# A decoder of twelve sub-layers on one core: a routed layer's first half placed beside the attention ahead of it, and two layers joined at their seam

## The chip, the cores and the metric

The kernel runs on one core of a Trainium2 chip. The core has a matrix engine (PE, TensorE), a vector engine (DVE, VectorE), an engine for activation functions (ACT, ScalarE), a general engine (POOL, GpSimd) and one that mainly issues transfers (SP, SyncE). Each takes its instructions in order from a queue of its own and waits for the others by semaphores. The metric is the device time of one execution in microseconds, the median of three runs.

## The reference

An input `x` of 32 sequences, 128 positions and 128 features goes through four decoder layers of three sub-layers each. Every sub-layer normalizes `x` and adds its result to `x`. Cut to the calls:

```
x = x + _L0_attn_ref(_layernorm(x), ...)        # state-space layer: convolution, gates, chunks of 64
x = x + _L0_xattn_ref(_layernorm(x), ctx, ...)  # cross attention, 8 heads of 64
x = x + _L0_ffn_ref(_layernorm(x), ...)         # mixture of 16 experts
x = x + _L1_attn_ref(...); x = x + _L1_xattn_ref(...); x = x + _L1_ffn_ref(...)
x = x + _L2_attn_ref(_layernorm(x), ...)        # one head
x = x + _L2_xattn_ref(ctx, _layernorm(x), ctx, ...)  # 16 heads, relative positions
x = x + _L2_ffn_ref(_layernorm(x), ...)         # top-1 mixture and a shared expert
x = x + _L3_attn_ref(_layernorm(x), ...)        # attention by sparsemax
x = x + _L3_xattn_ref(...); x = x + _L3_ffn_ref(...)
```

The mixture that matters here is the ninth sub-layer:

```
probs = softmax(x @ Wr)                         # 8 choices, 7 of them with an expert
p, ind = the largest of probs
out = 2.0 * p * sum over j < 7 of swiglu(x, Wu[j], Wg[j], Wd[j]) * (ind == j)
out = out + swiglu(x, Wu_s, Wg_s, Wd_s)         # the shared expert; hidden size 512
```

## The kernel before

`x` stays in SBUF as G=8 tiles, each one *group* of J=4 sequences: 128 positions on the partitions, 4x128 values beside each other. Each sub-layer is a function, `layer0` to `layer11`, called in order at the end of `program`; their matrices come as *units* of 768 KB in a pool of four buffers (tag `unit`). Other pools are named by what they hold: `bbig` (4 buffers) and `gbig` (3) of 2048 values a partition, `bmid` (5) and `gmid` (10) of 512, and in PSUM `ps`, `two` and `acc`, two buffers each.

The order of work is written out by hand. The wrapper `Ordered` (L181) keeps the instructions of VectorE, ScalarE and TensorE in the order of the program between `follow(T, A, V)` and `follow()`; that is why almost every row of the profile has the line L194 and groups are told apart by their tiles. GpSimd (`P`) and SyncE (`SY`) aren't wrapped; a scheduler places their instructions.

`layer0` works in rounds, one sequence in two chunks per round, G*J=32 in all. A round calls `first`, `second`, `third` and `weighted` for its chunks, and between them, by `go`, the next step of generators for other groups: `entry` (norm and turn), `conv` (convolution strand), `decays`, `gate`, and `joined` (gating, root mean square, projection, adding to `x`) for the group before. The loop runs from -9 to G*J+1, so that the first groups' preparation and the last group's `joined` are in rounds of their own.

`layer1` then prepares its first group and a half (`prepare`, `project_in`, `scores`, `project_values`) and runs 32 rounds of its own, with the next layer's preparation (`then`) in its last ones. `attention16` serves the 16-head attentions; it, too, works in rounds, one sequence each: transposes of the probabilities, scores of the next round, softmax, `weighted` (product with the values) of the round before, and one step of an iterator `others` handed to it. `layer7` is such an attention; its `others` were the leftovers of `layer6`.

`layer8` is the top-1 mixture. The tokens are dealt with in two halves (*sides*, four groups each). For one side: `ready` normalizes and `gate` makes logits, `route` picks the best expert by the routine `first_k`, `place` gives each token a row in DRAM so that an expert's rows stand in blocks of 256 (`TOKENS`), 14 tiles (`TILES`) in all; `send` scatters 128 tokens by an indirect transfer to `xs` (16 a side); `load(t)` gathers tile t's 768 KB of expert weights to a unit buffer; `rows` reads the tile's tokens back; `up` and `down` make the products and scatter the results to `ys`; `collect` reads them back and adds them. `shared` is a quarter of a group of the shared expert (16 pieces a side). `xs` and `ys` are filled with empty rows beforehand. `layer8_first` does all this for side 0, and routing and sending for side 1; side 1's tiles go to the list `beside`, which `layer9`, the sparsemax attention, takes up among its sorting steps.

Of the kernel before, what the change touches and what calls it, by code (L numbers as in the profile page):

```python
# [13 lines left out]
I8 = mybir.dt.int8  # L14
# [190 lines left out]
def program(ctx, tc, cols, x, ctxt, mask, drop, dfirst, dsmall, dwide, drows, dunits, dexperts, dconst, drel, dwq, out):  # L205
# [72 lines left out]
    SY.dma_start(out=cs, in_=dconst)  # L278
# [3 lines left out]
    for i in range(G):  # L282
# [3 lines left out]
        if i == 0:  # L286
            w0 = units.tile([128, cfirst.n], F32, tag="unit", name="w0")
            A.dma_start(out=w0, in_=dfirst)
            ww = const.tile([128, cwide.n], F32, name="ww")
            A.dma_start(out=ww, in_=dwide.to_broadcast([128, cwide.n]))  # L290
            wr = const.tile([1, crows.n], F32, name="wr")
            A.dma_start(out=wr, in_=drows)
# [26 lines left out]
    ctxT = [const.tile([128, 512], F32, name=f"ctxT{i}") for i in range(G)]  # L319

# [65 lines left out]
    def normed(i):  # L386

        xn = mid.tile([128, J, D], F32, tag="xn", name="xn", bufs=2)
# [7 lines left out]
        for j in range(J):  # L396
            P.tensor_scalar(xn[:, j, :], xg[i][:, j, :], mv[:, j, 0:1], rs[:, j : j + 1], ALU.subtract, ALU.mult)  # L397
# [270 lines left out]
    def layer0():  # L668
# [190 lines left out]
        def joined(g):  # L859

            ys, sq = [], []
            for b in range(2):
                y = bmid((128, J, 128))
# [8 lines left out]
            for y in ys:  # L872
                q = bmid((128, J, 128))
# [10 lines left out]
            ln = bmid((128, J, 128))  # L884
            A.copy(ln, op)
            yield
# [21 lines left out]
        for n in range(-9, G * J + 2):  # L908
# [46 lines left out]
            go(conv, g, c)  # L955
        follow()

    def layer1(then):  # L960
# [12 lines left out]
        def project_in(n):  # L973
            i, j = n // J, n % J
            at = slice(j * 128, (j + 1) * 128)
            if n % 2 == 0:
                keys[n // 2] = gbig((128, 2, 4, 256))
# [81 lines left out]
        follow(T, A, V)  # L1059
        prepare(0, 0)  # L1060
        prepare(0, 1)
        project_in(0)
        for c2 in range(2):
            for step in scores(0, c2):
                step()
        prepare(1, 0)
        project_in(1)
        project_values(0)
        for n in range(last + 1):
# [10 lines left out]
            if n < last:  # L1080
# [12 lines left out]
                weighted(n)  # L1093
                if j == 0 and 0 < i and i + 1 < G:
# [3 lines left out]
        follow()  # L1098
# [339 lines left out]
    def layer8(side):  # L1438

        N = G // 2  # L1440


        E = D + 1
        xs = dram.tile([TILES * TOKENS + HALF, E], F32, name=f"xs{side}", tag=f"xs{side}")
        ys = dram.tile([HALF + TILES * TOKENS, D], F32, name=f"ys{side}", tag=f"ys{side}")
        xs_rows = xs[0 : TILES * TOKENS].rearrange("(p n) e -> p n e", p=128)
        rows = TILES * TOKENS // 128
        number = small(rows)
        V.tensor_scalar(number[:, 0:1], K["row"], float(rows), float(HALF), ALU.mult, ALU.add)
        V.tensor_scalar(number, K["count"][:, 0:rows], number[:, 0:1], None, ALU.add)  # L1450
        for a in range(0, rows, 14):
            empty = bbig((128, 14, E))
            P.memset(empty, 0.0)
            V.tensor_copy(empty[:, :, D].bitcast(I32), number[:, a : a + 14])
            SY.dma_start(out=xs_rows[:, a : a + 14], in_=empty)
            if a == 0:
                SY.dma_start(out=ys[0:HALF].rearrange("(p n) d -> p n d", p=128), in_=empty[:, 0:1, 0:D].to_broadcast([128, HALF // 128, D]))
        xn_all = bbig((128, N, J, E))
        own = small(N * J)
        V.tensor_scalar(own, K["count"][:, 0 : N * J], 128.0, K["row"], ALU.mult, ALU.add)  # L1460
        V.tensor_copy(xn_all.rearrange("p n j e -> p (n j) e")[:, :, D].bitcast(I32), own)
# [3 lines left out]
        xnTs, sums, ins, mids = {}, {}, {}, {}  # L1465

        def ready(i):
            norm(xg[side * N + i], xn_all[:, i, :, 0:D])
# [482 lines left out]
```

## Time and profile before

| what | value |
|---|---|
| median of three runs | 3045.65 us (3045.08 to 3048.45) |
| profiled execution, its own time | 3068.78 us |
| its span, from first to last instruction | 3066.8 us |
| mean granted TensorE clock | 0.91 |
| busy: PE, DVE, ACT, POOL | 2563.0, 2086.1, 1529.3, 1007.4 us |
| bytes moved by DMA | 68.36 MB, mean 22 GB/s |
| attention of layer7, rounds 1 to 31 (VectorE's reciprocals of `weighted`) | 2039 to 2310 us |
| layer8 from the attention's last add to the last tile of side 0 | 2312.9 to 2504.4 us |

Busy times and shares are over the whole span. A row of a window has the start and end of a stretch and its length, then the busy time and the number of instructions of PE (matrix products), PEld (its weight loads), DVE, ACT and POOL, then the granted clock of PE (1 is full speed), the mean busy share of the DMA engines, and what they moved in GB/s. A row of the chain of waits has a start, a duration and what the kernel's end stood on at that time: an engine with its tile, "issue" where the engine waited for nothing that the profile shows, or "another core or an unknown queue". The kernel uses one core, so the latter is a queue here. All times of places are microseconds from the start of the span.

### The profile page before, as it was taken

What the parts mean: (1) busy time and instruction counts of PE and PEld (TensorE: products, weight loads), DVE (VectorE), ACT (ScalarE), POOL (GpSimd) and SP (SyncE); (2) the same over time, 40 slices, a digit from 0 to 9 for tenths busy, and PEclk for the clock granted to TensorE, in tenths of its full rate; (3) what the DMA queues carried; (4) which work ended last, traced back from release to release, by engine and by line L of the source; (5) the groups of instructions that cost most, each with busy time, mean ns of one, the idle gap of its engine ahead of it and who ended that gap; (6) DMA issues with size and microseconds to landing.
All of it is one profiled execution on the core that took longest, in us unless ns stands there. A gap on an engine that the chain in (4) does not pass through costs nothing.

```text
span 3066.8 us, 55735 instructions
## 1 busy us (share of the span) xinstructions
PE 2563.0 (84%) x22535; PEld 1638.7 (53%) x22554; DVE 2086.1 (68%) x4254; ACT 1529.3 (50%) x3540; POOL 1007.4 (33%) x1042
## 2 busy tenths in 40 slices
PE   4887878999989999999998999988886869885564
PEld 2555556777744445556664444445553657543333
DVE  4776756888878856667776555468894329777883
ACT  3554544444422246666664444467771225555563
POOL 3333332322310113235441000223433445424544
PEclk7877878999999999999998999979997989998777
DMA  3000000000000000000000000000003243100000
GB/s 109 2 2 2 2 23 4 8 5 5 1 21 1 1 32 2 5 9 9 12 2 15 1 1 1 1 1 2 1 6 124 84 147 114 55 18 14 21 11 21
DMA packets 50147, 68.36 MB, mean 22 GB/s; under 512 B 3681, under 2 KB 41570, under 8 KB 49762
## 3 DMA queue, kind: packets, MB, share of 16 engines
q1 hardware_dynamic: 42608, 33.84, 3.6%
q0 software_dynamic: 6848, 27.81, 2.7%
q8 instruction: 178, 2.92, 0.4%
q10 hardware_dynamic: 434, 3.14, 0.3%
q14 instruction: 79, 0.65, 0.1%
HBM read 51.11 MB, written 13.68 MB: 21 GB/s over the span
## 4 chain that ended last, share of the span: by engine, by line
PE 49%; DVE 31%; ACT 8%; POOL 6%; issue 3%; DMA 1%; another core or an unknown queue 1%; SPq 0%; POOLq 0%; DVEq 0%; ACTq 0%
PE ps L194 22%; PE two L194 15%; PE acc L194 13%; DVE bbig L194 13%; DVE s L194 9%; DVE bmid L194 4%; DVE gmid L194 3%; ACT bbig L194 3%; POOL xn L397 3%; ACT bmid L194 2%; ACT gmid L194 1%; DVE x L194 1%; POOL s L395 1%; ACT gbig L194 1%; POOL s L364 1%
## 5 line engine op out<-in xcount | busy, mean ns | idle before, releaser
L194 PE MATMUL ps<-cs,bbig 128*128 128x128 f32 x2208 | 326.6, 287 | 82.0 <-ACT bbig L194 34.4
L194 PEld LDWEIGHTS ps<-cs,bbig 128*128 128x128 f32 x2208 | 251.8, 145 | 187.2 <-ACT bbig L194 81.0
L194 ACT COPY bbig<-ps 128x512 f32<-128x512 f32 x416 | 228.2, 590 | 247.2 <-PE ps L194 246.9
L194 DVE TENSOR_REDUCE s<-two 128x8 f32<-128x1024 f32 (+1 forms) x192 | 234.2, 1220 | 123.7 <-PE two L194 122.6
L194 DVE TENSOR_TENSOR bbig<-bbig 128x256 f32<-128x256 f32 (+4 forms) x394 | 274.0, 749 | 1.3 <-ACT bbig L194 0.3
L194 PE MATMUL two<-xnT,u 128*128 128x512 f32 x512 | 260.0, 608 | 11.8 <-ACT bmid L194 6.3
L194 PE MATMUL acc<-bmid,u 128*128 128x512 f32 x448 | 238.2, 619 | 32.8 <-DVE bmid L194 31.4
L194 PE MATMUL two<-gbig,gmid 32*128 32x512 f32 (+1 forms) x1280 | 223.1, 570 | 3.1 <-ACT bbig L194 2.4
L194 DVE TENSOR_TENSOR bmid<-bmid,ps 128x512 f32<-128x512 f32 x192 | 130.1, 684 | 108.3 <-ACT bmid L194 89.2
L194 ACT ACTIVATE bbig<-two,s 128x256 f32<-128x256 f32 (+1 forms) x512 | 189.7, 419 | 24.5 <-DVE s L194 21.2
L477 POOL TENSOR_SCALAR gbig<-bmid,cs 128x512 f32<-128x512 f32 x96 | 148.7, 1564 | 160.0 <-ACT bmid L194 160.0
L194 ACT ACTIVATE bbig<-bbig 128x512 f32<-128x512 f32 (+1 forms) x160 | 128.1, 801 | 86.6 <-DVE bbig L194 86.1
L194 ACT ACTIVATE bmid<-two 128x512 f32<-128x512 f32 x104 | 61.7, 596 | 195.4 <-PE two L194 185.4
L194 PEld LDWEIGHTS acc<-bmid,u 128*128 128x128 f32 x448 | 81.3, 195 | 134.2 <-DVE bmid L194 77.5
L194 PEld LDWEIGHTS two<-xnT,u 128*128 128x128 f32 x512 | 91.4, 191 | 114.9 <-issue 56.0
L194 ACT ACTIVATE bmid<-two,ws 128x512 f32<-128x512 f32 x128 | 85.1, 686 | 110.0 <-PE two L194 109.8
L1020 POOL TENSOR_TENSOR bbig<-bbig,s 128x1024 f32<-128x1024 f32 x32 | 60.6, 1892 | 232.5 <-PE two L194 161.0
L194 ACT ACTIVATE bbig<-bbig,s 128x128 f32<-128x128 f32 x384 | 118.7, 387 | 27.4 <-DVE s L194 27.4
L194 DVE TENSOR_TENSOR bbig<-two,s 128x1024 f32<-128x1024 f32 (+1 forms) x128 | 122.6, 958 | 8.6
L489 POOL MEMSET val<- 128x512 f32 x72 | 39.4, 550 | 262.8 <-PE acc L194 261.8
L194 ACT COPY bbig<-bbig 128x256 f32<-128x256 f32 (+3 forms) x320 | 97.8, 375 | 49.2 <-DVE bbig L194 47.2
L194 PE MATMUL ps<-cs,xn 128*128 128x128 f32 x288 | 62.0, 307 | 70.7 <-POOL xn L397 25.1
(292 smaller groups left out, 5948.3 us busy)
## 6 DMA issues: line engine op xcount, KB each, us to landing
u<-in_units SPq DMA_DIRECT2D x10, 768.0 KB
gmid<-in_ctx SPq DMA_DIRECT2D x16, 256.0 KB
xs<-bbig SPq DMA_DIRECT2D x4, 903.0 KB
xt<-xs SPq DMA_DIRECT2D x28, 129.0 KB
x<-in_x SPq DMA_DIRECT2D x8, 256.0 KB
gmid<-in_mask SPq DMA_DIRECT2D x8, 256.0 KB
ys<-bbig SPq DMA_DIRECT2D x2, 1024.0 KB
gmid<-ys SPq DMA_DIRECT2D x8, 256.0 KB
```

Of the source, the lines that this page charges most:

```text
L194: d = f(*args, **kwargs)
L364: P.tensor_tensor(rs, rs, K["nhalf"], ALU.pow)
L395: P.tensor_tensor(rs, rs, K["nhalf"], ALU.pow)
L397: P.tensor_scalar(xn[:, j, :], xg[i][:, j, :], mv[:, j, 0:1], rs[:, j : j + 1], ALU.subtract, ALU.mult)
L477: P.tensor_scalar(o[:, n, :], k, K["n4"][:, n : n + 1], None, ALU.mult)
L489: P.memset(o, 0.0)
L1020: (V if c2 else P).tensor_tensor(pr[:, four, :], pr[:, four, :], bc(nm[:, four], 2, 256), ALU.mult)
```

## The change

The edit has three parts. First, the opening of `layer0`: the first group of `x` is loaded ahead of the constants, the quantized matrix `wq8` of layer11 is loaded behind the first units and cast in round 3 of `layer1`, and the rounds -9 to -3 give way to a hand-written order of `entry`, `decays` and `conv` steps. Second, the seam of `layer0` and `layer1`: `layer1` gives a generator `lead` with its preparation in seven steps, of which five are taken in the last five rounds of `layer0` and two between the steps of the last group's `joined`; the rest of that `joined` is handed to `layer1` as `others` and is drained by its round 2. Third, `layer8`: for side 0 the filling of `xs` and `ys`, norm, logits, picking, placing, the first load and the sending become a generator `ahead8`, whose step m is taken in round m+6 of layer7's attention, behind the six of `layer6`'s leftovers. Norms of this layer go by `normed`, in which GpSimd writes the normalized values. What remains, `layer8_rest`, makes two shared pieces and then the 14 tiles of side 0, with one shared piece and one step of side 1's routing beside a tile, side 1's placing at tile 5 and its sends spread from tile 6 on. The stages `turn`, `logits`, `gate`, `pick_one` replace `gate` and `route`, and work on one group at a time.

```diff
-    SY.dma_start(out=cs, in_=dconst)
...
         if i == 0:
+            SY.dma_start(out=cs, in_=dconst)
...
-    def normed(i):
-
-        xn = mid.tile([128, J, D], F32, tag="xn", name="xn", bufs=2)
+    def normed(i, xn=None):
+
+        if xn is None:
...
-            P.tensor_scalar(xn[:, j, :], xg[i][:, j, :], mv[:, j, 0:1], rs[:, j : j + 1], ALU.subtract, ALU.mult)
+            P.tensor_scalar(xn[:, j, 0:D], xg[i][:, j, :], mv[:, j, 0:1], rs[:, j : j + 1], ALU.subtract, ALU.mult)
...
-    def layer0():
+    def layer0(lead):
...
+            tile_of = gmid if g == G - 1 else bmid
...
-        for n in range(-9, G * J + 2):
+        go(entry, 0)
+        go(entry, 0)
+        go(entry, 0)
+        go(entry, 1)
+        go(entry, 0)
+        go(decays, 0)
+        go(conv, 0, 2)
+        go(entry, 1)
+        go(decays, 0)
+        go(conv, 0, 2)
+        go(conv, 0, 3)
+        go(conv, 0, 2)
+        go(conv, 0, 3)
+        go(entry, 1)
+        go(conv, 0, 2)
+        go(conv, 0, 3)
...
+        go(conv, 0, 1)
+        for n in range(-2, G * J):
...
+            if n >= G * J - 5:
+                next(lead)
+        go(joined, G - 1)
+        next(lead)
+        go(joined, G - 1)
+        next(lead)
+        go(joined, G - 1)
         follow()
-
-
-
-    def layer1(then):
+        return late[joined, G - 1]
...
-                keys[n // 2] = gbig((128, 2, 4, 256))
+                keys[n // 2] = (gbig if n else bbig)((128, 2, 4, 256))
...
+        def lead():
+            prepare(0, 0)
+            yield
+            prepare(0, 1)
+            yield
+            project_in(0)
+            yield
+            project_in(1)
+            yield
+            prepare(1, 0)
+            yield
+            steps = [step for c2 in range(2) for step in scores(0, c2)]
+            yield
+            steps[0]()
+            steps[2]()
+            project_values(0)
+            steps[1]()
+            steps[3]()
+            yield
+
+        def run(others, then):
+            follow(T, A, V)
+            for n in range(last + 1):
+                go_round(n, others, then)
+            follow()
+
+        def go_round(n, others, then):
...
+                next(others, None)
+                if n == 2:
+                    for _ in others:
+                        pass
+                if n == 3:
+                    V.tensor_copy(wq, wq8.bitcast(I8))
...
-    def layer8(side):
+    def layer8(side, tiles):
...
-        for a in range(0, rows, 14):
-            empty = bbig((128, 14, E))
-            P.memset(empty, 0.0)
-            V.tensor_copy(empty[:, :, D].bitcast(I32), number[:, a : a + 14])
...
-            norm(xg[side * N + i], xn_all[:, i, :, 0:D])
+
+            if i % per == 0:
+                t = tile_of(per)
+                own = small(per * J)
+                P.tensor_scalar(own, K["count"][:, 0 : per * J], 128.0, K["row"], ALU.mult, ALU.add)
+                if i:
+                    P.tensor_scalar(own, own, float(i * J * S), None, ALU.add)
+                P.tensor_copy(t.rearrange("p n j e -> p (n j) e")[:, :, D].bitcast(I32), own)
+                for k in range(per):
+                    xns[i + k] = t[:, k]
+            normed(side * N + i, xns[i])
+        def turn(i):
+            xnTs[i] = transposed(xns[i][:, :, 0:D], gmid(), A.copy)
+
+        def logits(i):
+            p = ps((128, J, 8))
+            for j in range(J):
+                mm(p[:, j, :], xnTs[i][:, j * 128 : (j + 1) * 128], W["f2_Wr"])
+            lgs[i] = small(J, 8)
+            A.copy(lgs[i], p)
...
+        def pick_one(i):
+            l, m = lgs.pop(i), small(J)
+            at = slice(i * J, (i + 1) * J)
             V.tensor_reduce(m, l, AX.X, ALU.add)
             V.reciprocal(m, m)
             V.tensor_tensor(l, l, bc(m, 2, 8), ALU.mult)
-            first_k(l, 8, 1, ssel, N * J)
+            first_k(l, 8, 1, ssel[:, at])
...
+    def empty_rows():
+
+        rows = TILES * TOKENS // 128
+        number = small(rows)
+        P.tensor_scalar(number[:, 0:1], K["row"], float(rows), float(HALF), ALU.mult, ALU.add)
+        P.tensor_scalar(number, K["count"][:, 0:rows], number[:, 0:1], None, ALU.add)
+        for a in range(0, rows, 11):
+            n = min(11, rows - a)
+            empty = units.tile([128, n, E], F32, tag="unit", name="empty")
+            P.memset(empty, 0.0)
+            P.tensor_copy(empty[:, :, D].bitcast(I32), number[:, a : a + n])
+            for xs, ys in both:
+                SY.dma_start(out=xs[0 : TILES * TOKENS].rearrange("(p n) e -> p n e", p=128)[:, a : a + n], in_=empty)
...
+        ready, turn, logits, gate, pick_one, place, send, shared, load, rows, up, down, collect = layer8(
+            0, (2, lambda n: units.tile([128, n, J, E], F32, tag="unit", name="xn8")))
...
+            fill = empty_rows()
+            for n in range(3):
+                put(n, next, fill)
+            for i in range(N):
+                for k, f in enumerate((ready, turn, logits, gate, pick_one)):
+                    put(3 + 3 * i + k, f, i)
+            put(17, place)
+            put(17, load, 0)
+            for c in range(N * J):
+                put(18 + c // 2, send, c)
...
+        later = [lambda i=i, c=c: shared(i, c) for i in range(N) for c in range(4)]
+        later.pop(0)()
+        later.pop(0)()
         up(0)
         for t in range(TILES):
             if t + 3 < TILES:
                 load(t + 3)
             if t + 2 < TILES:
                 rows(t + 2)
+            if t < N:
+                ready2(t)
             if t + 1 < TILES:
                 up(t + 1)
+            if 0 < t <= N:
+                turn2(t - 1)
+                logits2(t - 1)
+                gate2(t - 1)
+                pick_one2(t - 1)
+            if t == N + 1:
+                place2()
             down(t)
-            if t == 0:
-                place2()
-            for _ in range(2 if t > 1 else 0):
-                if later:
-                    later.pop(0)()
+            if later:
+                later.pop(0)()
+            if t > N + 1:
+                for c in range((t - N - 2) * N * J // (TILES - N - 2), (t - N - 1) * N * J // (TILES - N - 2)):
+                    send2(c)
...
     load_units(0, 1, 2, 3, 4)
-    layer0()
+    SY.dma_start(out=wq8, in_=dwq)
+    lead1, run1 = layer1()
+    rest0 = layer0(lead1)
     load_units(5)
     lead2, run2 = layer2()
-    layer1(lead2)
+    run1(rest0, lead2)
     load_units(6, 7)
     lead3, run3 = attention16(layer3(), layer4())
     run2(lead3)
...
     bias7, layer = layer7()
     lead7, run7 = attention16(layer)
     run5(bias7, lead7)
-    run7(last6, iter(()))
-    layer8_first()
+    ahead8, run8 = layer8_first()
+
+    def beside7():
+        yield from last6
+        yield from ahead8
+
+    run7(beside7(), iter(()))
+    run8()
```

## The prediction

> **What bounds the kernel now.** I read the page's busy shares and chain first.
>
> ```profile
> PE 2563.0 (84%) x22535; PEld 1638.7 (53%) x22554; DVE 2086.1 (68%) x4254; ACT 1529.3 (50%) x3540; POOL 1007.4 (33%) x1042
> ...
> PE 49%; DVE 31%; ACT 8%; POOL 6%; issue 3%; DMA 1%; another core or an unknown queue 1%; SPq 0%; POOLq 0%; DVEq 0%; ACTq 0%
> ```
>
> TensorE is busy 84% of the 3066.8 us span, so at most some 500 us of it is idle, and a change that only moves work can win what is idle at its own places. The second view is therefore the table of windows at the three places that the diff touches. Its columns are the stretch, its length, the busy time of PE, PEld, DVE, ACT and POOL, the granted clock, the DMA share and GB/s.
>
> ```profile
> 0.00:48.70 48.70, 12.31 (x28) 6.34 (x29) 19.36 (x59) 14.22 (x26) 14.65 (x19) 0.87 0.50 172
> 441.80:490.90 49.10, 31.71 (x146) 24.29 (x145) 19.10 (x57) 13.27 (x38) 18.30 (x21) 0.62 0.09 27
> 491.00:539.30 48.30, 48.06 (x415) 38.06 (x416) 38.05 (x58) 23.15 (x78) 7.90 (x5) 1.00 0.02 7
> 2195.00:2230.60 35.60, 29.79 (x384) 19.63 (x380) 28.80 (x49) 26.43 (x71) 14.93 (x19) 0.90 0.01 2
> 2230.60:2266.00 35.40, 28.16 (x412) 18.77 (x400) 34.65 (x91) 28.00 (x76) 20.40 (x28) 1.00 0.01 2
> 2330.00:2360.00 30.00, 16.72 (x32) 6.87 (x32) 12.62 (x57) 3.65 (x7) 21.30 (x24) 0.61 0.10 34
> 2401.50:2470.00 68.50, 51.17 (x266) 44.76 (x266) 21.79 (x49) 16.61 (x34) 36.90 (x45) 0.85 0.35 112
> 2470.00:2504.40 34.40, 34.40 (x214) 31.69 (x213) 8.25 (x12) 10.77 (x23) 19.40 (x26) 1.00 0.59 184
> ```
>
> To be seen: before the first chunk (first row) no engine works half of the time; between layer0 and layer1 (second row) PE runs at clock 0.62 and what it does is mostly waiting or slow, while the rounds behind it (third row) are PE work without a gap; the attention of layer7 (rows 4, 5) has 6 to 7 us free on PE and DVE in each group of four rounds; and layer8 (rows 6 to 8) loses time until its last six tiles, which run PE full, 5.57 us each. The chain of waits names what layer8 stands on in its middle:
>
> ```profile
> 2427.77 6.74 issue
> 2434.61 6.24 another core or an unknown queue
> 2440.87 0.61 ACT h L194
> ...
> 2451.52 8.13 another core or an unknown queue
> ```
>
> **Part A, the opening: -5 us (0 to -10).** First product of a chunk at 48.70. VectorE stands 2.27 us for the quantized weight `wq` at 25.75; that cast moves to a round of layer1, so 2.3 us go. VectorE's 4.89 us wait for `ws` until 16.4 keeps its place in the order, so loading `x` ahead of the constants gains nothing behind it. The new order starts entry(1) early and interleaves the four convolution strands by two; the busiest engine had 19.36 us of work in 48.7, so this is latency. I take 2.7 us for it, from nothing to 8. The moved `wq8` load stays behind the first three weight loads on SP's queue, so nothing is delayed there.
>
> **Part B, layer0 into layer1: -27 us (-15 to -33).** Before, the tail of group 7 and then layer1's preparation stand in a row, from the last state sums to layer1's first round, 441.80 to 490.90: 49.1 us. In the order of instructions after, only this stays between the last states (443.5) and that round: 16 products of `w0` with the joined tile (2.0 us in full-clock rows), 16 mean-square products (1.9), two score blocks (2 x 1.05), two value products (2 x 1.0), 16 transposes (2.6): 10.6 us, plus about 2.5 of waits for copies, so 455 if nothing came earlier. What moved into layer0's last five rounds costs PE 8 transposes (1.3) and twice 16+8 projection products (2 x 3.0): 7.3 us, of which PE's 5.2 idle us in 430 to 445 (9.76 busy of 15.00) can cover a part; I charge 5. Round 0 is then at 460, 31 earlier. The joined tail (ACT 2.2 us, DVE 2.6, POOL 3.9) now rides in layer1's rounds 0 to 2, which PE fills (48.06 of 48.30), with DVE at 38 and POOL at 8: it is hidden by PE, I charge 2 for its place in the orders, and 2 for bubbles where DVE and ACT evict in two layers' order. 31-4=27. Both context loads stand ahead of the load of u3, which waits for the release of `w0`, so SP holds nothing that round 0 needs; without that cover the third group's context would be late, needed five rounds (58 us) later. Lower end: the rounds of layer0 before 430 are PE-full, and all 7.3 us plus the serial evictions (about 8) are paid. The cost of writing the joined tail in another pool's tile is nothing.
>
> **Part C, layer8: -44 there, +20 in the attention ahead of it, -24 in all.** From the end of the attention (2312.9) to the last tile's product (2504.4) it takes 191.5 us. After, routing, placing, 16 sends and the first three weight loads lie before 2312.9. PE's own work left, at full clock: 16 shared pieces (four of them 10.83 us in 2373 to 2384, transposes included) 43; 14 tiles at 5.57, 78; the other half's four turns and logits (0.66+0.97) 6.5; placing 0.6: 128 us. Added: four routing steps among the tiles, stalls in the feed, and side 1's sends.
>
> Routing steps. Each brings one Exp between Silus. ACT loads a table in 1.28 us (2321.91, 2400.92, 2402.54 in the trace): 9 loads in place of 3, 7.7 us of ACT more, ACT having 16.6 of 68.5 us busy. The Trainium skill, ScalarE: Activation LUTs, section What ACT_TABLE_LOAD costs, puts a switch at 2.66 us, the load of 1283 ns and a drain of 1380 ns; its rule, to batch functions of one set, speaks against this change. Two switches a step are 2.6 us by the row, 5.3 by the page; about one tile's product (3.57 us) lies ahead on PE as cover. I charge 2 us a step, 8 in all (0 to 16, the upper end by the page).
>
> Feed. Before, ACT stood 6.80, 5.70 and 8.21 us with no engine to wait for, while weights were gathered; the page lists an instruction queue of 178 packets and 2.92 MB, 16.4 KB each. The Trainium skill (Runtime: NRT & Kernel Launch, section Instruction fetch mechanics) says that an engine's instruction memory is refilled in 16 KiB blocks over its own queue and that this is mostly hidden. The packets agree; the hiding doesn't here, if these gaps are fetches, which no row names. By the page these 20.7 us would be 0, by the rows they return. With shared pieces beside tiles, a tile takes about 8.1 us and the gather needs 1 MB per 8.1 us, 124 GB/s where 184 was moved in the last row, so I charge 6 (0 to 20). Side 1's last 13 sends stand in one lump on POOL ahead of load(10): 13 x 1.26 = 16.5 us, two tiles, and three buffers are loaded ahead: 5 us (0 to 12). 128+8+6+5=147, so -44 (-25 to -58). The half-clock of 2330 to 2360, where PE waited for routing, goes with it.
>
> The attention. Per group of side 0: VectorE's stats were already beside the attention (the fifth window: 91 instructions where the fourth has 49, 5.9 us more, and the length 35.4 against 35.6, though at clock 1.00), so new is gate and pick, about 4 us by the rows of routing (0.29, 1.22 and 0.16 to 0.3 each at a quarter of the size), in three rounds; PE's transposes and logits 1.6; POOL's norm 0.23+1.05+4x0.78=4.4. A group has 6.8 us free on VectorE. Most is absorbed, but each is queued ahead of the next softmax step: 1.5 us a group, 6 in all. Placing, one round (23): about 5 us of VectorE (2330.64 to 2335.5 before, with waits for PE): 5. PE's and POOL's own: 4. Then POOL's order: all 16 sends and three loads, 19 x 1.26 = 24 us, stand ahead of group 7's expanded keys (6.2 us). Before, these keys were made at 2257.65 to 2263.85 and needed at about 2283 (scores of round 28). Sends that begin at 2257 end at 2281, keys at 2287.5: 5 us late (0 to 10); PE's scores wait, then VectorE's softmax. The row-number copies behind them, waiting for the rows to land, stand ahead of group 7's values, which are due a round and a half later: 0. Sum 6+5+4+5=20 (5 to 35). The fill writes of xs, 3.6 MB, lie beside rounds with a DMA share of 0.01: nothing; at 2298 to 2316 before they also cost nothing visible.
>
> **Sum.** -5-27-24=-56 on the profiled execution, whose own time is 3068.78 us (span 3066.8), 23 above the median. Differences are carried over as they are: 3045.65-56 = **2990 us**, likeliest between 2970 and 3008.
>
> **Rivals.** (1) Everything hides: the fifth window's free 5.9 us holds for gate and pick (attention +5), the feed has slack (layer8 -55), so -5-27-50=-82, 2964 us. For it: DVE's free time; against it: POOL's lump. (2) The feed stays: the fetch gaps return and POOL's lump holds load(10) (layer8 -25), and the attention, whose chain is in good part VectorE's, pays what is put into it (+28): -5-27+3=-29, 3017 us. For it: rounds 1 to 5, which carry the last layer's leftovers, took 50.4 us and not 35.6. (3) Slower: POOL's sends in the attention. If each of the 19 takes p us beside a busy VectorE, the keys are late by 19p-19 us; at 1.26 that is the 5 above. It eats the 56 us from p=4.2 on; at p=5 it is 76, 71 more than charged, and the time 3061. Against it: 0.96 and 0.30 us in each row of the sends, with VectorE at work in half of them. (4) No change: the new orders leave the seam and the opening as they are, and layer8's gain is paid in the attention.
>
> **How the numbers follow.** Forecast 0.50, (1) 0.14, (2) 0.24, (3) 0.08, (4) 0.04. What a measurement of this kernel can tell from no change is about 0.2%, 6 us. Faster 0.88, same 0.04, slower 0.08. The range leaves out (3), (4) and the outer parts of (1) and (2): 2962 to 3028.
>
> **What would show it.** Right: first chunk's product at about 44; layer1's first round 45 to 60 us after the last convolutions of layer0 become 15 to 20; the length from the attention's last add to the last tile of side 0 at 140 to 155 us with PE's clock at 1; the rounds 9 to 27 of layer7 about 15 longer in sum, one gap of some 5 us on PE in round 27 with POOL's keys as releaser. Wrong: ACT gaps without releaser among the tiles above 20 us in sum; a wait for `we` at the tenth tile above 12; rounds of layer7 longer by more than 35; or layer1's first round less than 20 us earlier, relative to the last states.

## The result and the profile after

The changed kernel takes 3011.24 us (median of four executions, 2997.87 to 3012.24), against 3045.86 for the kernel before in the same comparison: a ratio of 0.9875, 95% interval 0.9846 to 0.9903. The forecast was 2990 us, with a range of 2962 to 3028. So the direction and the range held, and of the 56 us that were forecast about 35 arrived. A later comparison with more executions gave 3006.85 against 3044.68.

The profiled execution of the changed kernel took 2997.87 us and is the fastest of its four; that of the kernel before took 3068.78, 23 above its median. The two traces differ by 71 us where the medians differ by 35. This is why the stages below are read from several traces, and not from these two alone.

Busy shares and the chain of waits of the changed kernel, from its page:

```profile
PE 2537.5 (85%) x22535; PEld 1623.6 (54%) x22554; DVE 2093.3 (70%) x4296; ACT 1538.0 (51%) x3560; POOL 1029.8 (34%) x1085
...
PE 49%; DVE 31%; ACT 8%; POOL 7%; issue 3%; DMA 1%; POOLq 0%; DVEq 0%; ACTq 0%
```

The work is the same; VectorE and GpSimd have a little more to do. "Another core or an unknown queue" has gone from the chain. The windows that answer to those of before, with the same columns (start:end, length, busy PE, PEld, DVE, ACT, POOL, granted clock, DMA share, GB/s):

```profile
0.00:51.00 51.00, 23.66 (x74) 13.21 (x74) 25.58 (x76) 19.96 (x41) 17.77 (x25) 0.83 0.46 164
425.20:446.50 21.30, 16.02 (x86) 12.02 (x85) 15.99 (x45) 8.11 (x28) 11.01 (x12) 0.76 0.16 50
447.00:470.00 23.00, 22.56 (x197) 17.80 (x196) 17.30 (x28) 12.56 (x40) 5.54 (x4) 1.00 0.00 1
2252.40:2260.70 8.30, 2.67 (x13) 0.93 (x12) 1.22 (x4) 2.74 (x7) 8.22 (x12) 0.64 0.65 232
2301.70:2330.00 28.30, 25.39 (x135) 19.60 (x132) 10.85 (x32) 11.21 (x21) 9.80 (x13) 1.00 0.25 79
2330.00:2390.00 60.00, 57.40 (x282) 43.19 (x281) 29.05 (x84) 25.53 (x46) 34.65 (x44) 0.97 0.34 106
2390.00:2445.00 55.00, 47.07 (x219) 33.76 (x217) 11.87 (x18) 12.85 (x27) 25.82 (x32) 0.94 0.41 132
```

To be seen: the first 51 us, which end with the first score blocks (these came at 64.3 before), now hold nearly twice the PE work that the first 48.7 held before; between the last state products of layer0 (425.2) and layer1's first round there are 21.3 us where before there were 49 (row 2), and then PE is full (row 3); near the end of layer7's attention (row 4) everything waits for GpSimd, which is busy throughout; and in layer8 (rows 5 to 7) PE is busy 130 of 143 us with its clock near 1.

The stages, as differences of the starts of named instructions in each trace (first score blocks of layer0; its last gate product but one; the scaling of probabilities in layer1's rounds 4 and 31; VectorE's reciprocals of the weighted products 0, 8, 24 and 31 of layer7; the first read of side 0's results), in us:

| stage | before | after | after, once more | opening undone | loads only | seam undone | layer8 undone | turn later | keys first |
|---|---|---|---|---|---|---|---|---|---|
| to the first score blocks | 64.3 | 51.0 | 51.3 | 63.2 | 59.3 | 49.6 | 50.9 | 49.6 | 50.9 |
| layer0's rounds | 343.5 | 334.4 | 337.5 | 342.2 | 336.0 | 346.9 | 340.8 | 342.0 | 341.3 |
| to layer1's round 4 | 119.3 | 97.6 | 97.6 | 103.2 | 103.2 | 117.9 | 97.6 | 101.4 | 97.6 |
| layer1, rounds 4 to 31 | 328.0 | 328.0 | 328.0 | 328.1 | 328.1 | 328.0 | 328.0 | 328.0 | 328.0 |
| layers 2 to 6 | 1172.8 | 1173.1 | 1174.5 | 1175.1 | 1175.2 | 1172.6 | 1177.7 | 1173.6 | 1173.9 |
| layer7, rounds 0 to 8 | 87.3 | 84.5 | 83.4 | 85.3 | 85.3 | 85.4 | 83.1 | 85.4 | 83.4 |
| layer7, rounds 8 to 24 | 142.5 | 174.1 | 173.8 | 173.0 | 174.0 | 174.1 | 142.5 | 165.5 | 172.9 |
| layer7, rounds 24 to 31 | 52.2 | 56.2 | 55.7 | 55.7 | 56.2 | 56.1 | 52.1 | 55.7 | 53.5 |
| to side 0's results | 200.6 | 146.0 | 143.8 | 143.7 | 145.7 | 145.8 | 186.8 | 144.5 | 143.7 |
| the rest | 556.3 | 551.2 | 553.9 | 551.4 | 551.4 | 557.4 | 552.0 | 553.7 | 552.7 |

Most stages repeat within about 2 us from trace to trace of kernels that are equal there. Three don't: layer0's rounds (334 to 347), the layers 2 to 6 (1173 to 1178) and the rest (551 to 557). They vary as much between kernels that are equal there as between the two of the change. The trace of before was on the long side in two of them and had a long layer8 besides. Two more differed once without an edit there: the seam, at 101.4 us in turn later, whose layer0 and layer1 are those of the changed kernel, and layer7's rounds 0 to 8, at 87.3 before and at 83.1 with layer8 undone.

What varies in layer0's rounds can be read from their windows, here in the changed kernel and in turn and keys, whose layer0 is the same:

```profile
50.96:385.40 334.44, 270.10 (x4698) 175.38 (x4698) 242.04 (x462) 178.49 (x330) 130.71 (x126) 0.86 0.01 3
50.92:395.70 344.78, 279.56 (x4698) 180.44 (x4698) 241.24 (x462) 178.41 (x330) 129.57 (x126) 0.83 0.01 3
```

The same 4698 products take 270.10 us at a mean clock of 0.86 and 279.56 at 0.83. In all 14 traces, PE's busy time there lies between 269.5 and 283.2 us, while the length less that time stays between 63.6 and 65.2. So the scatter of this stage is the time of PE's products, and not waiting.

### The profile page after: what moved, and what is told of

The parts are those of the page before. It is cut to its first block, busy times and chain, and to the rows that moved or that the text cites. A ratio compares the mean times of both kernels' runs of the same rounds, so it can differ in the third digit from the quotient of the medians.

```text
span 2996.1 us, 55816 instructions
## 1 busy us (share of the span) xinstructions
PE 2537.5 (85%) x22535; PEld 1623.6 (54%) x22554; DVE 2093.3 (70%) x4296; ACT 1538.0 (51%) x3560; POOL 1029.8 (34%) x1085
## 4 chain that ended last, share of the span: by engine, by line
PE 49%; DVE 31%; ACT 8%; POOL 7%; issue 3%; DMA 1%; POOLq 0%; DVEq 0%; ACTq 0%
PE ps L194 21%; PE two L194 15%; DVE bbig L194 13%; PE acc L194 13%; DVE s L194 9%; DVE bmid L194 4%; DVE gmid L194 3%; ACT bbig L194 3%; POOL xn L402 3%; ACT bmid L194 2%; POOL s L400 1%; POOL xs L1608 1%; ACT gmid L194 1%; DVE x L194 1%; POOL s L368 1%
## 5 line engine op out<-in xcount | busy, mean ns | idle before, releaser
L402 POOL TENSOR_SCALAR xn<-x,s 128x128 f32<-128x128 f32 x152 | 122.3, 816 | 5.3 <-PE ps L194 1.4
```

The costliest lines, as they stand in the source:

```text
L402: P.tensor_scalar(xn[:, j, 0:D], xg[i][:, j, :], mv[:, j, 0:1], rs[:, j : j + 1], ALU.subtract, ALU.mult)
```

## The experiments

**The changed kernel again.** No edit.

> The changed kernel once more, to see where its executions differ by 14 us (2997.87 against 3010.67 to 3012.24). Theory: the difference lies in layer0's rounds, whose groups take 54.7 us or 49 to 53 us by the trace; then the median is 3011 within 2, and a profile near 3011 has layer0's groups at 54.7 throughout. Rival: it lies in layer8, where expert weights are gathered; then layer0 looks the same in both profiles and layer8 is some 14 us longer.

Measured: median 3006.85 (3000.62 to 3021.86, six executions), and 3044.68 for before (23 executions, 3033.59 to 3055.97). Its trace, of 3001.19 us, has layer0's rounds 3 us longer than the first one and layer8 2 us shorter. Traces of the later kernels show layer0's rounds at up to 347 us. So the place is the likely one, but the median that the theory named (3011 within 2) missed, and there are not two modes: the rounds take many values between 334 and 347. No trace at 3011 or above was taken of this kernel itself.

**Opening undone.**

```diff
+    SY.dma_start(out=cs, in_=dconst)
...
         if i == 0:
-            SY.dma_start(out=cs, in_=dconst)
...
-        go(entry, 0)
-        go(entry, 0)
...
-        for n in range(-2, G * J):
+        for n in range(-9, G * J):
```

The quantized matrix is again loaded and cast by layer9's code.

> The changed kernel with the opening of before (constants first, rounds from -9, the quantized matrix loaded and cast at layer9). By the two profiles, in which the first chunk's score blocks start at 63.30 and 50.01, the opening is worth 13 us: 3024. My prediction charged 5: 3016. Rival, the opening's gain also sets the pace of layer0's rounds: 22 us and more, 3033.

Measured: 3026.84 (13 executions, 3013.12 to 3038.53), 20.0 above the changed kernel of the same comparison. The first score blocks are 12 us later (63.2 against 51.0 and 51.3). The seam to layer1 is 5.6 us longer as well (103.2 against 97.6), which neither theory had. Layer0's rounds, 342 us, lie within what other kernels show there, so that rival isn't supported.

**Loads only.** The loads and the moved cast kept, the hand-written steps taken back (of the diff above, the lines from the first `go(entry, 0)` on).

> The changed kernel with the order of loads and the moved cast of the quantized matrix kept and the hand-written order of layer0's first steps taken back (rounds from -9). Theory: of the 13.3 us by which the first score blocks come earlier, the loads and the cast give 4 (1.6 from the small weights' landing, 2.3 from the cast), the order 9: first score blocks at about 59. Rival, the prediction's halves (2.3 and 2.7) were right for the loads and the rest comes from the loads too: first score blocks at 54 or earlier.

Measured: first score blocks at 59.28: loads and cast give 3.9 us (63.16 to 59.28), the order 8.3 (to 50.96). The median is 3021.66 (11 executions, in another comparison than the changed kernel's). The seam is at 103.2 again. The loads are thus not its cause, but that the hand-written steps are isn't shown either. Most of these 5.6 us are one place where the same 161 products run at another clock, here in the changed kernel, in loads only and in turn later, which has the hand-written steps:

```profile
407.50:413.40 5.90, 5.90 (x161) 4.74 (x160) 3.05 (x6) 1.94 (x2) 1.51 (x3) 0.95 0.01 3
416.90:426.40 9.50, 9.50 (x161) 7.55 (x160) 3.18 (x6) 3.12 (x6) 2.01 (x4) 0.51 0.01 2
413.20:422.70 9.50, 9.50 (x161) 7.55 (x160) 3.17 (x6) 3.12 (x6) 1.98 (x4) 0.51 0.01 2
```

PE doesn't wait in any of the three. Of the kernels with the new seam, both without the hand-written steps have the slow stretch, and of the ten traces with them only turn later; that is a hint at most. VectorE's rows of this kernel in the opening (start, duration, instruction, in brackets the idle time ahead and what ended it):

```profile
28.98 2.30 DVE L194 SCALAR_TENSOR_TENSOR gmid<-bmid,w,gmid 128x508 f32<-128x508 f32 x3 [1.36 <-ACT gmid L194]
...
34.89 3.18 DVE L194 SCALAR_TENSOR_TENSOR gmid<-bmid,w,gmid 128x508 f32<-128x508 f32 x3 [2.16 <-ACT gmid L194]
...
49.12 0.29 DVE L194 TENSOR_TENSOR dts<-ps,ww 128x128 f32<-128x128 f32 x1 [5.23 <-PE ps L194]
```

and the row of the changed kernel that takes the place of the first ones:

```profile
23.31 6.37 DVE L194 SCALAR_TENSOR_TENSOR gmid<-bmid,w,gmid 128x508 f32<-128x508 f32 x6 [3.03 <-ACT gmid L194]
```

Two convolution strands stand together, six instructions without a gap, where one strand at a time waits for ScalarE between its threes; and the second group's first steps no longer wait 5.2 us at 49.

**Seam undone.**

```diff
-        for n in range(-2, G * J):
+        for n in range(-2, G * J + 2):
-            if n >= G * J - 5:
-                next(lead)
-        go(joined, G - 1)
-        next(lead)
...
+        follow()
```

Layer1 prepares its first groups behind layer0, as before.

> The changed kernel with layer0's end and layer1's start as before. By the profiles the offset grows from 21.3 at 414 us to 44.0 at 525 us, 22.7: 3034. The prediction's 27 gives 3038. Rival, layer0's last rounds are full and pay for what is put into them: 10, 3021.

Measured: 3026.24 (11 executions), 19.4 above the changed kernel; the stretch to layer1's round 4 is 117.9 us against 97.6, 20.3. The rival is out; the theory's 22.7 was 2 us too much and the prediction's 27 seven.

**Layer8 undone.** Layer7's attention and layer8 as before, the other parts of the change kept:

```diff
-    run7(beside7(), iter(()))
-    run8()
+    run7(last6, iter(()))
+    layer8_first()
```

> The changed kernel with layer7's attention and layer8 as before. By the profiles the attention is 35.8 us longer and layer8 54.4 shorter, 18.6 net: 3030. The prediction's 44 less 20 gives 24: 3035. Rival, nothing is left of it outside this one profile: within 5 of 3011.

Measured: 3011.77 (six executions, 3008.20 to 3026.18), only 4.9 above the changed kernel, which by medians of six is not clear of the scatter. By stages the attention takes 31.3 to 31.6 us more in rounds 8 to 24 and 3.6 to 4.1 more in rounds 24 to 31 with the change, and the stretch to side 0's results 41 to 43 less, 5 to 8 net. The 54 us of the two first traces were too many because of the trace of before: ScalarE's waits among the tiles, in the kernel before,

```profile
ACT h L194 <- PE two L194: 17.8, 9, 4.9
ACT h L194 <- remote: 13.9, 2, 8.2
ACT h L194 <- issue: 11.0, 2, 6.8
```

(us in all, times, longest) and with layer8 undone, over the corresponding stretch:

```profile
ACT h L194 <- PE two L194: 35.0, 18, 7.0
ACT yt L194 <- DMA ys<-yt,at: 6.1, 2, 3.3
```

The waits without an engine are not there, and the stage is 186.8 us instead of 200.6, though layer8's code is the same. So they don't come with every execution of it; what they were is open.

**Keys first.** On GpSimd, side 0's sends behind the last group's keys (in `send`), the row-number copies behind its values (in `rows`):

```diff
-                put(18 + c // 2, send, c)
+                put(20 + c // 3, send, c)
...
+                tc.add_manual_dep(d.ins, newest["keys"].name, info, reason="the last group's keys first")
...
+                tc.add_manual_dep(d.ins, newest["val"].name, info, reason="the last group's values first")
```

> The changed kernel with side 0's sends begun two rounds later, three a round, and ordered on GpSimd behind the last group's expanded keys (and the row-number copies behind its values). Theory: in the changed kernel's trace VectorE waits 7.05 us at 2260.67 for scores whose keys GpSimd made only at 2251.75, behind the sends; without it the stretch from round 24 to 31 of layer7's attention falls from 56 to about 50 us, and the time by 5 to 7. Rival: the sends end later, so that the first tiles' rows or the last group's values are late and layer8 or the attention's end gives it back: no change within 3.

What it takes away, in the changed kernel: GpSimd's rows

```profile
2248.21 0.95 POOL L1608 DMA_INDIRECT xs<-xn,pos  x1 [0.30 <-issue]
2249.47 0.99 POOL L1635 DMA_INDIRECT we<-in_experts,wrow  x1 [0.31 <-DMA xs<-xn,pos]
2250.76 0.96 POOL L1635 DMA_INDIRECT we<-in_experts,wrow  x1 [0.30 <-DMA xs<-xn,pos]
2251.75 6.67 POOL L482 TENSOR_SCALAR gbig<-bmid,cs 128x512 f32<-128x512 f32 x4
```

and the waits from 2252 to 2262 us:

```profile
DVE bbig L194 <- PE two L194: 7.0, 1, 7.0
...
PE two L194 <- POOL gbig L482: 5.6, 1, 5.6
```

Measured: 3004.30 (four executions; before in this comparison 3046.10), rounds 24 to 31 at 53.5 us instead of 55.7 to 56.2. The wait for the keys is gone and another came, which is the rival's second half. Waits of this kernel from 2272 to 2286 us:

```profile
PE acc L194 <- POOL val L667: 3.7, 1, 3.7
DVE s L194 <- PE acc L194: 3.7, 1, 3.7
```

The last group's values now stand behind all 16 sends. More than half of the gain went there.

**Turn later.**

```diff
-                    put(3 + 3 * i + k, f, i)
+                    put(3 + 3 * i + k + (k > 0), f, i)
```

> The changed kernel with turn, logits, gate and pick each one round further behind a group's norm. Theory: PE's transposes stand in its queue ahead of the next round's scores and wait for GpSimd's norm, which waits behind the expanded keys (6.2 us): PE waits 0.4 us per quarter in rounds 10 to 11, falls to half clock, and VectorE waits 4.33 us at 2084.26; without this 3 us a group go, so rounds 8 to 24 fall from 174 to about 162 us. Rival: the cost of these rounds is VectorE's own added instructions: no change within 3 us there.

Measured: 2993.88 (four executions, 2992.68 to 3001.03; ratio to before 0.9825, interval 0.9779 to 0.9872), rounds 8 to 24 at 165.5 us, 8.6 less. The theory asked for 12 and the rival for at most 3; the theory is the nearer in this pair of traces. In two other pairs of kernels, which differ by this edit and by the order of the sends or of the keys behind it (keys first against turn and keys; picks by pairs against three together), the stage falls by only 3.0 and 4.2. This round of the changed kernel shows what was lost, the first in which a group is turned:

```profile
2078.70:2091.30 12.60, 11.02 (x110) 8.01 (x109) 8.10 (x20) 8.56 (x23) 2.65 (x7) 0.73 0.01 1
```

12.6 us where the same round takes 8.7 with layer8 undone, with PE's clock down to 0.73. Rows of that round, and the row of layer8 undone that answers to the second:

```profile
2078.53 0.33 PE L194 MATMUL ps<-cs,xn 128*128 128x128 f32 x1 [0.44 <-POOL xn L402]
...
2082.07 2.09 PE L194 MATMUL two<-gbig,gmid 32*128 32x512 f32 x8
...
2084.26 1.23 DVE L194 TENSOR_TENSOR bbig<-two,gbig 128x1024 f32<-128x1024 f32 x1 [4.33 <-PE two L194]
...
2088.30 1.14 PE L194 MATMUL two<-gbig,gmid 32*128 32x512 f32 x8
```

The group's four transposes wait for GpSimd's norm, three of them some 0.45 us each; the scores behind them then take 2.09 us instead of 1.14, and VectorE waits 4.33 us for them.

**Picks by pairs.** The logits of two groups stand in one tile, and softmax and pick are made on it at once:

```diff
-            first_k(l, 8, 1, ssel[:, at])
+            first_k(l, 8, 1, ssel[:, at], pair * J)
```

> The changed kernel with side 0's softmax and pick made for two groups at once: by the rows some 4.7 us of VectorE per group become about 5 per pair, 8 to 9 us less in rounds 8 to 24. Theory: these instructions stand between one round's weighted product and the next round's softmax and are paid in full: 174 falls to 165 us. Rival: VectorE waits for PE in these rounds anyway and half or more of its work is absorbed: 174 falls by 4 us or less.

Measured: 3005.71 (four executions); rounds 8 to 24 at 172.8 us, 1.3 less. VectorE's work there fell only from 144.0 to 139.7 us: a pair takes 5.3 us by the rows, about as counted, and so a single group took 3.7 on the mean (10.6 and 4.3, by four) and not 4.7. Half of the saving was not there, and of the rest most went into other waits. By its numbers the rival won: here, with the turn still in the way, taking 4.3 us of VectorE's work out gave 1.3.

**Three together.** Keys first, turn later, picks by pairs in one kernel, with no other edit.

> The three edits together (keys first, turn one round later, picks by pairs). If the three causes are separate, rounds 8 to 24 fall from 174 to about 153 us, rounds 24 to 31 from 56 to 50, and the median from 3007 by 25 to about 2982. If they share one slack the sum is less: 2992. Rival: no gain, 3007.

Measured: 2994.27 (four executions), rounds 8 to 24 at 168.6 and 24 to 31 at 52.6 us. The sum is less, as the second guess had it, and turn later alone is 3 us shorter in rounds 8 to 24.

**Turn and keys.** As turn later, and eight sends behind the last keys, eight behind the last values:

```diff
+                what = "keys" if c < 8 else "val"
+                tc.add_manual_dep(d.ins, newest[what].name, info, reason="the last group's keys and values first")
...
-                put(18 + c // 2, send, c)
+                put(20 + c // 4 if c < 8 else 18 + c // 2, send, c)
```

> Turn one round later and, on GpSimd, side 0's first eight sends behind the last group's keys and the other eight behind its values; picks one group at a time. In keys_first the values were 4 us late behind all 16 sends, which gave back most of the 6.6 us of the keys. Theory: rounds 8 to 24 as in turn_later, 165.5 us; rounds 24 to 31 down from 56 to about 51; median 2994 less 4, 2990. Rival: the second eight sends end after the attention and layer8 starts late: the stretch to the collecting grows from 144 by 4 or more, and the median stays at 2994.

Measured: 2995.70 (five executions). Rounds 24 to 31 fall to 49.1 us, less than without any sends there (52.1); the stretch to side 0's results stays at 144.4, so the rival is out. But rounds 8 to 24 are at 169.9 in this trace, 4 more than in turn later, and the median is not better. PE was busy 130.8 us of them for the same 1556 products, at a clock of 0.86, against 125.9 at 0.89: these 4 us, too, are the time of PE's products. Why the clock differed stays open, as does why rounds 24 to 31 are shorter than without sends.

**Spread.** As turn and keys, with each pick in three rounds and placing in three (two more `yield` in each):

```diff
+            yield
...
-                    put(3 + 3 * i + k, f, i)
+            for i, r in enumerate((3, 5, 8, 10)):
+                put(r, ready, i)
+                put(r + 2, turn, i)
+                put(r + 3, logits, i)
+                put(r + 4, gate, i)
+                steps = pick_one(i)
+                for k in range(3):
+                    put(r + 5 + k, next, steps)
```

> As turn_keys, and each pick in three pieces in three rounds, placing in three too, norms at other distances. Theory: VectorE waits about 1.3 us for scores in each round; a piece of at most 2.5 us fits there in part, one of 4.3 or 6 us sticks out. Rounds 8 to 24 then fall from 165 to about 153 us, median 2980. Rival: the rounds pay for every instruction that VectorE gets, wherever it stands: 165 stays within 3.

Measured: 3002.59 (five executions), rounds 8 to 24 at 169.8 us: nothing gained against turn and keys (169.9), and neither the theory's 153 nor the rival's 165 within 3. The distances of the norms changed in it too, so it says only that cutting the pieces smaller doesn't bring 12 us.

**Pick twice.** As turn later, with the ranking made twice for side 0:

```diff
             first_k(l, 8, 1, ssel[:, at])
+            if side == 0:
+                first_k(l, 8, 1, ssel[:, at])
```

> As turn_later, with the ranking of side 0's picks (first_k, about 2.5 us of VectorE a group by the rows) made twice, so that 10 us of VectorE work are added in rounds 8 to 24 and nothing else. In turn_later VectorE is idle 23 us of that stretch's 165.5, as idle as without any routing (22 of 142.5). Theory: the idle time is waiting that follows from the chain, and each microsecond put on VectorE is paid: 165.5 becomes 175. Rival: the idle time takes it up: 169 or less.

Measured: 3007.57 (four executions), 13.7 above turn later (in another comparison), and rounds 8 to 24 at 175.2 us, 9.7 longer, for 9.1 us more of VectorE. The rows for rounds 8 to 24 in the four kernels, one fence each: with layer8 undone,

```profile
2078.25:2220.76 142.51, 117.15 (x1506) 78.89 (x1506) 120.51 (x223) 108.93 (x288) 63.43 (x82) 0.92 0.01 2
```

the changed kernel,

```profile
2068.62:2242.74 174.12, 134.00 (x1557) 88.50 (x1557) 143.97 (x315) 112.56 (x300) 91.90 (x118) 0.85 0.03 10
```

turn later,

```profile
2079.88:2245.38 165.50, 125.90 (x1556) 85.94 (x1556) 142.45 (x315) 112.66 (x300) 91.49 (x118) 0.89 0.03 10
```

and pick twice:

```profile
2074.58:2249.74 175.16, 128.13 (x1556) 87.42 (x1556) 151.55 (x339) 112.66 (x300) 91.66 (x117) 0.86 0.03 9
```

VectorE's idle time (length less its busy time) is 22.0, 30.2, 23.1 and 23.6 us. It is about the same with no routing, with routing and the turn later, and with the ranking doubled: it isn't slack that takes work up. Turn and keys showed that this stage can differ by 4 us without an edit, so the single rounds tell more. The four rounds that hold a pick take 11.6, 12.1, 10.5 and 17.2 us in turn later and 13.9, 14.3, 12.7 and 19.4 here, 2.2 to 2.3 more each for 2.3 us of VectorE; against turn and keys it is 1.8 to 2.2. So work that is put in is paid nearly in full. In these two traces, with the turn out of the way, routing costs 23 us for 21.9 of VectorE, and the turn 8.6; by the other two pairs the turn is 3.0 and 4.2.

## Why the prediction was right or wrong

**The opening (-5, at most -10).** More: 12 to 13 us at the first score blocks. The product that the forecast set at 44 starts at 35.05, 14.5 earlier than before (49.55; the 48.70 of the forecast is its weight load). The term that failed is the order of the first steps, taken at 2.7 us and measured at 8.3; loads and cast gave 3.9 where 2.3 was charged, since the small weights, for which VectorE waits at about 15, land 1.6 us earlier (14.85 against 16.42). I had written that an earlier load gains nothing behind that wait. The 5.6 us at the seam are products at a lower clock and can't be booked to the opening with certainty.

**The seam (-27).** The mechanism held, the size is 20. The step that failed is the sum of what stays behind the last states. From 425.2 to the first round at 446.5 it takes 21.3 us, where 10.6 of products and 2.5 of waits were counted (from 443.5 that is 456.6, and not the 455 of the forecast). The sum has two score blocks where four stand there, two of the first sequence and two of the second: 2.1 us at its own price. The waits for copies were too few, and the rates were those of full clock. PE's rows there (timeline of the changed kernel):

```profile
434.39 1.22 PE L194 MATMUL two<-bbig,gmid 64*128 64x256 f32 x2 [5.28 <-ACT bbig L194]
435.54 3.58 PE L194 MATMUL ps<-w,gmid 128*128 128x128 f32 x16
...
441.78 3.54 PE L194 MATMUL ps<-cs,bbig 128*128 128x128 f32 x16
```

PE waits 5.28 us for the exponentials of layer1's first scores, which wait for VectorE, which has the joined tile's sums ahead of them in its order; and after the gap the 16 projection products take 3.58 us instead of 2.0, the 16 transposes 3.54 instead of 2.6, at a clock of 0.66 to 0.76. The lead was placed early enough for its products and not for its softmax.

**Layer8 (-44).** The size is right, 41 to 43 against the same stage of an otherwise equal kernel, by two errors that cancel. The 191.5 us from which it was taken held ScalarE's 6.80, 5.70 and 8.21 us, which another execution of the same layer8 doesn't show: with layer8 undone the stage is 13.8 us shorter. And the 147 us for what remains were 10 too many: from the attention's last add (2301.7) to the last tile (about 2439) it took 137. The charge for the feed (6) was for the same gaps; none is in the changed kernel's traces among the tiles. The Trainium skill (Runtime: NRT & Kernel Launch, section Instruction fetch mechanics) says that refills are mostly hidden, which fits these other traces; whether the gaps in the first one were refills is shown by nothing. The lump of sends (5) was sized well: the load for the tile that PE waits for stands behind the last of them on GpSimd, and PE stood 4.26 us (4.0 to 4.3 in eight traces with this layer8):

```profile
2393.09 0.97 POOL L1608 DMA_INDIRECT xs<-bbig,pos  x1 [0.16 <-issue]
...
2394.42 1.00 POOL L1635 DMA_INDIRECT we<-in_experts,wrow  x1 [0.15 <-issue]
...
2399.92 1.19 PE L194 MATMUL two<-xT,we 128*128 128x256 f32 x2 [4.26 <-DMA we<-in_experts,wrow]
```

The routing steps cost little of their 8 us: eight table loads came where nine were counted, and six of them, 1.28 us each, fall in 60 us in which PE was busy for 57.4. The drain that the Trainium skill adds to each (ScalarE: Activation LUTs, section What ACT_TABLE_LOAD costs) doesn't show on ScalarE either: the next activation starts at once, 0.01 us behind the load.

```profile
2338.14 1.28 ACT L194 ACT_TABLE_LOAD   x1
2339.43 0.23 ACT L194 ACTIVATE s<-s 128x32 f32<-128x32 f32 x1
```

**The attention (+20, to 35).** The step that failed. It cost 35 to 36 us (31.5 in rounds 8 to 24, about 4 from 24 on), which reaches the forecast's own sign of being wrong, over 35. The keys' 5 us held: 5.6 measured, part of it won back in the last rounds. The amount of VectorE's work was about right: 23.5 us were added, where four picks of 4 us and 5 for placing had been counted. What was wrong is "most is absorbed", 1.5 us a group: put into these rounds it is paid nearly in full. I took it from one window of before (2230.6 to 2266), where 5.9 us more of VectorE lay in the same length; that window had a clock of 1.00 and the other 0.90, and it held single statistics of 0.2 us. In that window VectorE was busy for 34.65 of 35.40 us, so the "6 to 7 us free" that I read in both windows are in the first alone; the second has 0.75. A window with more work at another clock is no test of slack; pick twice is one. The turn's wait was not in the sum at all: PE's transposes stand ahead of the next scores in its order and wait for GpSimd, and what comes of it is 3.0 to 8.6 us by the pair of traces, most of it slower products and not the waits themselves (in the changed kernel against turn later 8.1 of the 8.6 us are PE's busy time, 134.0 against 125.9). What stands behind a moved instruction in its queue was asked for GpSimd, and not for PE.

So the net of the third part is 5 to 8 us and not 24, the seam gave 7 less than its 27, and the opening, with more than its 5, made up for some of it. That the total lies within the range is in part this luck. Undone one at a time, the three cost 20.0, 19.4 and 4.9 us, 44 in sum, where the whole is 37.8 in the same comparison; with executions that scatter by some 7 us about their medians, and stages that change with PE's clock, these are not more exact than that.

Of the rivals, the second (3017) came nearest: its half on the attention was right, at +35 for its 28, its half on the feed was wrong, and it had the opening and the seam as the forecast had them. Its total is near by luck. The rival that was to be slower, GpSimd's sends, failed at its price: they took 0.96 and 0.30 us each in the attention too.

A version that beats both kernels came out: one more round between norm and turn, 2993.88 us. It was compared with the kernel before (0.9825) and not side by side with the changed one, whose ten executions took 2997.87 to 3021.86.

## What to carry to other kernels

Idle time of an engine in a chained loop need not be slack: before putting work beside such a loop, put a little of it in twice and see whether the loop gets longer. When a step is moved into another stage's order, list for every in-order engine what its instructions wait for and who is queued behind them; one round of distance between producer and consumer was worth about as much as the whole of the move. And before a stage's gain is taken from one trace, look at a second trace of the same kernel: of 71 us between the first two traces here, half was in the executions.

## What the runs showed of the hardware

The 23 executions of the kernel before in one comparison differed by 22 us (3033.59 to 3055.97). The 14 traces, of kernels that make the same products in layer0's rounds, show 13 us between them there (333.8 to 346.9), all of it PE's time for the same 4698 products at mean clocks of 0.82 to 0.86. Layer1's rounds 4 to 31, which keep PE full at a clock of 1.00, took 327.96 to 328.10 in every trace. The same 161 products took 5.90 us at a clock of 0.95 in one trace and 9.50 at 0.51 in another of the same code. Gaps on PE are followed by slower products (3.58 us for 16 instead of 2.0 behind the 5.28 us gap), so that a loop with gaps can multiply small shifts; what makes the clock differ from one execution to the next was not tested.

Indirect sends on GpSimd took about 0.96 us with 0.30 between them, beside the attention as beside the tiles. On ScalarE a table load took 1.28 us, and the next activation started 0.01 us behind it.
